# Two graph layers on one core: queries' sums as seven products of combined quarters

## The chip, the cores and the metric

The kernel runs on one core of a Trainium2 chip. A core has five engines that each work through their own instruction list in order: TensorE (PE in the profile; its weight loads are shown as PEld), VectorE (DVE), ScalarE (ACT), GpSimd (POOL) and SyncE (SP), which here only issues DMAs. The metric is the device time of one execution, in microseconds.

## The reference, cut to what matters

The input `x` is 16 graphs of 1024 nodes with 256 channels, `adj` one 1024 x 1024 matrix shared by all. The first layer, with `fea` the normed input with channels first:

```python
c_adj = jnp.mean(fea, axis=1)
diff = c_adj[:, None, :] - c_adj[:, :, None]
A = jnp.abs(jnp.abs(jax.nn.sigmoid(diff) - 0.5) - 0.5) * 2.0
A_s = (A + jnp.transpose(A, (0, 2, 1))) * 0.5
Wg = adj[None, :, :] * A_s
g = jnp.einsum('bcn,bnm->bcm', fea, Wg)          # <- the queries' sums
g = jax.nn.relu(g * para.reshape(1, C, N))
q = jnp.transpose(g, (0, 2, 1)).reshape(B, N, h, hd).transpose(0, 2, 1, 3)
kv = (x @ kv_w).reshape(B, N, 2, h, hd).transpose(2, 0, 3, 1, 4)
...
attn = jax.nn.softmax(jnp.einsum('bhnd,bhmd->bhnm', q, k) * scale, axis=-1)
out = jnp.einsum('bhnm,bhmd->bhnd', attn, v)
```

For each graph the 256 x 1024 matrix `g` is a product of the 256 x 1024 features with a 1024 x 1024 weighted graph `Wg`, which is different for every graph. The second layer multiplies the normed sum by a normalised adjacency (`A_hat`, the same for all graphs), then by W1, takes a batch norm over all graphs, a ReLU, W2, and a second batch norm.

## The kernel before

`layers(False)` does the first layer and the second up to W1; `second("f")` does the batch norms, W2 and the output. (`layers(True)` and `second("s")` are a safer path that is taken only if a sum of exponentials overflows; it doesn't run on this data.) All matrices are FP32.

**The order of the work.** The program is recorded in the order in which the code emits it, with no reordering, and every engine keeps that order. `attention` (line 806) walks over 16 graphs of 16 steps each. A step emits, in this order: `scores` of one group of nodes (`sc`, two PSUM tiles, and the exponentials `p` on ScalarE), the transposes of a finished unit (`ot`), additions of `p` into `acc` on VectorE, the products with the values of the step before (`o`), at the end of a unit the `sums` with four reciprocals on VectorE, and then pieces of a background. The background of graph b, `background(b)` at line 612, is a generator; it makes the queries, keys and values of graph b + 1, the gathering with `A_hat` (`aggregate`, PE `pa`) and W1 (`hidden`, PE `py`) of graph b - 1, and the norm and the weights' start (`prepare`) of graph b + 2. Each `yield 1.71` is one piece of TensorE work of that many microseconds; a step takes pieces until the sum of costs reaches the share of `total` (line 822) that is due. `weave` puts side generators beside a main one, one piece of each side per piece of the main. `soon(action)` emits an action after the next piece. A piece that yields `TOP` stops the step, and the next one begins with the background directly behind the scores.

**The queries.** `weigh` (line 363) makes `Wg` in 8 pieces of 256 rows x 512 columns (two row blocks of 128; 4 KB per partition). Piece i goes by two slots: in the first the DMA of `adj` for piece i + 1 is issued, VectorE finishes piece i - 1 (line 381, `w * adj`) and ScalarE begins piece i (line 394, two instructions), in the second ScalarE takes the tanh (line 402). `AHEAD = 6` slots run ahead of `queries`, the others beside it, one for each of its pieces. `queries` (line 407) multiplies each piece with both halves of the channels (k = 0, 1) into two PSUM banks, over the eight row blocks, for the left and then the right half of the columns: 2 x 8 x 2 = 32 products of 128 x 128 by 128 x 512. `product` splits each into two matmuls of 64 columns of weights; the profile shows two instructions for each matmul. At the end of a half VectorE multiplies by `para` (line 432) and ScalarE takes the ReLU (line 435). The pieces live in four buffers (`w`), as do those of `adj`, and the pieces of `A_hat` that `aggregate` loads are in the `adj` buffers too.

**The seven products.** `aggregate` already works with seven products of quarters: `graph` makes, once, from the normalised adjacency the four blocks and three combinations, in DRAM (`aht_d`), and `combine` and the functions behind each product combine quarters of the features and add the results. `h` is normed features, `h_a` for the first layer, `h_b` for the second; its quarters are a11, a12 (first channels, first and second half of the nodes) and a21, a22.

**The buffers around it.** `load_adj` and `load_adj_t` load pieces of `adj`; `columns_of` and `broadcast_row` make a row of 1024 values out of a column by transposes (tiles `cb`, PSUM `cbp`); `dbc` is such a row of the degrees, for `graph`. PSUM tiles of all these products are the two banks of `ps_mm` (`bank`, line 142). `y` tiles hold W1's results on the way to DRAM, in four buffers of the pool `py`. W2 (`w2`) is loaded in `degrees` (line 206) into memory of its own.

The head of the run, before `attention`, makes the keys, values and queries of graph 0:

```python
run(weave(keys_values(0), (8 - AHEAD, islice(weighers[0], AHEAD))))
load_x(1)
run(weave(queries(0), (0, weighers[0]), (5, Norm(1, True).all())))
attention()
run(aggregate(B - 1), hidden(B - 1))
```

## Time and profile before

| what | value |
|---|---|
| median of 3 runs | 2697.38 us (2697.13 to 2699.46) |
| the profiled execution, whole | 2699.94 us |
| its span in the profile | 2698.1 us |
| TensorE clock granted, mean | 0.988 |
| `pg` matmuls (queries' sums), busy | 457.1 us, 2048 instructions |
| `pa` matmuls (`aggregate`), busy | 346.0 + 57.8 us, 1536 + 256 instructions |
| one graph of the steady part (graphs 2 to 13) | 148.3 us |
| head, up to the first scores | 61.9 us |
| first product of the second part | begins at 2422.2 us |

The span is what lies between the first and the last recorded instruction of that execution. An engine's busy time is the sum of its instructions; in a row of a group the columns are the code's line, the engine, the operation, what it writes and reads, the shapes, the count, the busy time, the mean duration in nanoseconds, and the idle time of that engine just before such instructions with what ended it.

### The profile page before, as it was taken

The numbers are of one execution on the slowest core, as the hardware profiler recorded it, in microseconds if no ns is written. First come the engines' busy times: TensorE is split into PE (matmuls) and PEld (weight loads), VectorE is DVE, ScalarE is ACT, GpSimd is POOL, SyncE is SP. The second block draws the span as 40 slices with busy tenths as digits, with TensorE's granted clock in tenths as the row PEclk, the third lists the DMA queues.
The fourth block names the chain that finished last, engine by engine and source line by source line (L and its number), as shares of the span: only waits on it lengthen the run. The fifth ranks groups of instructions, "written<-read, shape, count | busy, mean of one in ns | idle before, by whom it ended". The sixth has DMA issues, their size and how long they took to land.

```text
span 2698.1 us, 32021 instructions
## 1 busy us (share of the span) xinstructions
PE 2620.7 (97%) x12106; PEld 968.3 (36%) x12106; DVE 1742.3 (65%) x2624; ACT 1292.3 (48%) x1845; POOL 363.2 (13%) x428
## 2 busy tenths in 40 slices
PE   7999999999999999999999999999999999989994
PEld 3333333333333333333333333333333333324443
DVE  5767666666666656666666666566666666656675
ACT  5653444536363544445363635444453634335544
POOL 0016000000000100000000001000000001026653
PEclk9999999999999999999999999999999999999997
DMA  4416414243332424142423324241424213355549
GB/s 156 159 58 225 161 53 164 86 148 103 107 116 98 141 80 158 51 168 83 150 100 109 114 98 141 84 155 51 168 82 152 99 63 118 113 215 187 202 182 364
DMA packets 128613, 355.05 MB, mean 132 GB/s; under 512 B 11969, under 2 KB 32961, under 8 KB 122305
## 3 DMA queue, kind: packets, MB, share of 16 engines
q1 hardware_dynamic: 109120, 278.44, 30.3%
q0 software_dynamic: 19328, 74.46, 7.3%
q8 instruction: 98, 1.61, 0.2%
q14 instruction: 67, 0.54, 0.1%
HBM read 278.41 MB, written 74.45 MB: 131 GB/s over the span
## 4 chain that ended last, share of the span: by engine, by line
PE 93%; DMA 3%; DVE 2%; issue 2%; ACT 1%; POOL 0%; SPq 0%; POOLq 0%; DVEq 0%; ACTq 0%
PE sc L704 18%; PE o L745 18%; PE pg L149 16%; PE pa L149 13%; PE py L149 7%; PE m_f L1017 7%; PE pk L149 4%; PE pv L149 4%; PE sums L762 2%; DMA out_dram<-xo_f 2%; PE ot L798 1%; PE htp L352 1%; PE cbp_c L192 1%; DMA y_d<-y 0%; DVE acc L734 0%
## 5 line engine op out<-in xcount | busy, mean ns | idle before, releaser
L712 ACT ACTIVATE p<-sc 128x1024 f32<-128x1024 f32 x512 | 496.4, 1021 | 700.8 <-PE sc L704 700.6
L734 DVE TENSOR_TENSOR acc<-acc,p 128x1024 f32<-128x1024 f32 x384 | 471.2, 1227 | 133.8 <-ACT p L712 112.5
L704 PE MATMUL sc<-q,k 64*128 64x512 f32 x2048 | 510.6, 617 | 0.5 <-ACT p L712 0.5
L745 PE MATMUL o<-p,v 128*64 128x512 f32 x2048 | 496.1, 605 | 0.0
L149 PE MATMUL pg<-w,h_a 128*64 128x512 f32 x2048 | 457.1, 596 | 7.5 <-DVE q L432 7.5
L149 PE MATMUL pa<-aht,h_b 128*64 128x512 f32 x1536 | 346.0, 592 | 2.7 <-DMA aht<-aht_d 2.7
L704 PEld LDWEIGHTS sc<-q,k 64*128 64x128 f32 x2048 | 176.6, 186 | 321.9 <-issue 270.3
L149 PEld LDWEIGHTS pg<-w,h_a 128*64 128x64 f32 x2048 | 148.2, 138 | 301.8 <-issue 281.7
L771 DVE RECIPROCAL inv<-sums 128x128 f32<-128x128 f32 x256 | 223.7, 921 | 24.6 <-PE sums L762 24.6
L149 PE MATMUL py<-at,w 128*64 128x512 f32 x1024 | 230.8, 592 | 2.1 <-ACT y L564 2.1
L745 PEld LDWEIGHTS o<-p,v 128*64 128x64 f32 x2048 | 124.3, 136 | 286.1 <-issue 285.9
L394 ACT ACTIVATE w<-cbc,csum 128x512 f32<-128x512 f32 x256 | 170.2, 714 | 74.3 <-PE pg L149 74.2
L731 DVE TENSOR_TENSOR acc<-p,p 128x1024 f32<-128x1024 f32 x64 | 78.5, 1226 | 194.8 <-ACT p L712 194.8
L381 DVE SCALAR_TENSOR_TENSOR w<-w,adj 128x1024 f32<-128x1024 f32 x128 | 156.5, 1223 | 54.7 <-ACT w L402 54.7
L149 PEld LDWEIGHTS pa<-aht,h_b 128*64 128x64 f32 x1536 | 110.6, 137 | 216.6 <-issue 204.9
L564 ACT ACTIVATE y<-py,vec 128x512 f32<-128x512 f32 x128 | 87.6, 684 | 188.4 <-PE py L149 155.1
L565 POOL DMA_DIRECT2D y_d<-y x128 | 70.7, 553 | 685.1 <-ACT y L564 681.9
L402 ACT ACTIVATE w<-w 128x1024 f32<-128x1024 f32 x128 | 134.8, 1053 | 1.7
L149 PEld LDWEIGHTS py<-at,w 128*64 128x64 f32 x1024 | 74.0, 137 | 147.8 <-issue 131.3
L149 PE MATMUL pv<-kvw,ht 128*64 128x256 f32 x1024 | 116.2, 379 | 0.4 <-DVE v L469 0.4
L82 POOL TENSOR_SCALAR lnsm_b<-mv_b 128x4 f32<-128x4 f32 x32 | 7.3, 230 | 805.2 <-DVE mv_b L277 805.1
L802 DVE TENSOR_TENSOR x<-ot,x 128x512 f32<-128x512 f32 x64 | 44.2, 691 | 110.6 <-PE ot L798 109.8
(133 smaller groups left out, 2526.4 us busy)
## 6 DMA issues: line engine op xcount, KB each, us to landing
aht<-aht_d SPq DMA_DIRECT2D x224, 512.0 KB, 4.2
adj<-in_adj_dram SPq DMA_DIRECT2D x128, 512.0 KB, 4.2
y_d<-y POOLq DMA_DIRECT2D x128, 256.0 KB, 2.8
yin_f<-y_d SPq DMA_DIRECT2D x32, 1024.0 KB, 6.3
x<-in_x_dram SPq DMA_DIRECT2D x32, 512.0 KB, 4.7
para<-in_para_dram SPq DMA_DIRECT2D x64, 256.0 KB, 4.1
x_d<-x POOLq DMA_DIRECT2D x16, 1024.0 KB, 4.2
xo_f<-x_d SPq DMA_DIRECT2D x32, 512.0 KB, 8.5
```

The lines of the kernel that those rows point to most:

```text
L149: nc.tensor.matmul(dst[r], left[:, r], right, start=start, stop=stop)
L381: nc.vector.scalar_tensor_tensor(w, w, 1.0, a, op0=ALU.add, op1=ALU.mult)
L394: nc.scalar.activation(w[:, t, :], cbc[:, q * FB : (q + 1) * FB], AF.Abs, bias=csum[:, th * TH + t : th * TH + t + 1], scale=-1.0,)
L402: nc.scalar.activation(made[i], made[i], AF.Tanh, scale=-0.5 / C)
L564: nc.scalar.activation(y, made, AF.Identity, bias=b1[:, j : j + 1])
L704: nc.tensor.matmul(sc[:, e, :], ks[b][k][r, m * P : (m + 1) * P], qs[b][k][r, f * FB : (f + 1) * FB], start=True, stop=True,)
L712: nc.scalar.activation(pr, sc, AF.Exp)
L731: nc.vector.tensor_add(self.acc, self.held, pr)
L734: nc.vector.tensor_add(self.acc, self.acc, pr)
L745: nc.tensor.matmul(self.o[r, :], vs[b][k][:, m, r], pr[:, e, :], start=(m == 0), stop=(m == NT - 1),)
L771: nc.vector.reciprocal(self.inv[:, c], self.pt[:, c])
L1017: nc.tensor.matmul(made, left[:, j, :], right[:, j, :], start=(j == 0), stop=(j == JH - 1))
```

## The change

`queries` now computes the four quarters of `g` (two halves of the channels, two halves of the columns) from seven products of a combined quarter of the features with a combined quarter of `Wg`, four row blocks each: 28 products in place of 32. The quarters of `Wg` are four blocks of two pieces each; the combinations are made in place, over the pieces and over the quarters of h_a, by `take`, `combine` and the functions `first` to `seventh`, on GpSimd, for graphs 0 and 2 on VectorE. All eight pieces are held at once (pool `p8`, tag `w`), which `aggregate` now uses for its loads too, five ahead instead of three. Beside this, `adj` has three buffers instead of four, `cb` uses the `y` buffers, `dbc` an `ht` buffer, and W2 is loaded at the start of the second part. The weights are made two slots per piece of the main generator (`double`), with `AHEAD = 9`. The background of graph 0 is put in another order, with the keys and values ahead of the queries, and `load_x(2)` moves to the head.

```diff
     nc.sync.dma_start(out=vec, in_=vecs)
-    w2 = const.tile([P, HC, C], F32, name="w2")
     b1, g1, be1 = (vec[:, i * HC : (i + 1) * HC] for i in range(3))
...
         p3 = st.enter_context(tc.tile_pool(name=f"p3_{kind}", bufs=3))
+        p8 = st.enter_context(tc.tile_pool(name=f"p8_{kind}", bufs=8))
         p4 = st.enter_context(tc.tile_pool(name=f"p4_{kind}", bufs=4))
...
+        def double(slots):
+            for _ in slots:
+                next(slots, None)
+                yield 0.0
         def bank(name):
...
         def load_adj(q, th, name):
-            t = p4.tile([P, TH, FB], F32, tag="adj", name=name)
+            t = p3.tile([P, TH, FB], F32, tag="adj", name=name)
             nc.sync.dma_start(
...
         nc.sync.dma_start(out=kvw, in_=kv_w.rearrange("(k p) j -> p k j", p=P))
-        dbc = big.tile([P, N], F32, name="dbc")
-        w1 = big.tile([P, CC, H1], F32, name="w1")
         rows = big.tile([P, NH, NT], F32, name="rows")
...
             for g in range(NT // 4):
-                cb = p2.tile([P, 4, P], F32, tag="cb", name=f"cb_{name}_{g}")
+                cb = py.tile([P, 4, P], F32, tag="y", name=f"cb_{name}_{g}")
                 nc.vector.tensor_copy(
...
         def load_adj_t(t, name):
-            tile_ = p4.tile([P, N], F32, tag="adj", name=f"{name}_{t}")
+            tile_ = p3.tile([P, N], F32, tag="adj", name=f"{name}_{t}")
             nc.sync.dma_start(out=tile_, in_=adj_t[t * P : (t + 1) * P, :])
...
         deg_sm = big.tile([P, 6, NT], F32, name="deg")
+        w1 = big.tile([P, CC, H1], F32, name="w1")
         row, diag, col, deg, tmp_deg, dinv = (deg_sm[:, i, :] for i in range(6))
...
             nc.sync.dma_start(out=w1, in_=w1_t.rearrange("(k p) j -> p k j", p=P))
-            nc.sync.dma_start(out=w2, in_=w2_t.rearrange("(k p) c -> p k c", p=P))
             nc.vector.tensor_reduce(row, rows.rearrange("p q t -> p t q"), AX.X, ALU.add)
...
-        def graph():
+        def graph(dbc):
...
                     cols = slice(part * HB, (part + 1) * HB)
-                    a = p4.tile([P, 2, NH, HB], F32, tag="adj", name=f"au_{t}_{part}")
+                    a = p3.tile([P, 2, NH, HB], F32, tag="adj", name=f"au_{t}_{part}")
                     for n in range(2):
...
                         load()
-                    w = p4.tile([P, TH, FB], F32, tag="w", name=f"w_{b}_{q}_{th}")
+                    w = p8.tile([P, TH, FB], F32, tag="w", name=f"w_{b}_{q}_{th}")
                     made.append(w)
...
-        AHEAD = 6
+        AHEAD = 9
+        def quarters(tag, b):
+            h = hs[tag, b]
+            HT = NT // 2
+            return [h[:, n * HT : (n + 1) * HT, c * P : (c + 1) * P] for c in (0, 1) for n in (0, 1)]
+        def combine(tag, b, engine):
+            a11, a12, a21, a22 = quarters(tag, b)
+            s1s[tag, b] = p1.tile([P, NT // 2, P], F32, tag="s1", name=f"s1_{tag}_{b}")
+            engine.tensor_add(s1s[tag, b], a21, a22)
+            engine.tensor_sub(a21, a11, a21)
...
-            h = hs["a", b]
+            engine = nc.vector if b in (0, 2) else nc.gpsimd
+            combine("a", b, engine)
+            a11, a12, a21, a22 = quarters("a", b)
+            s1 = s1s["a", b]
             qs[b] = [p4.tile([P, N], F32, tag="q", name=f"q_{b}_{k}") for k in range(CC)]
...
+            c11, c12, c21, c22 = (
+                qs[b][k][:, q * FB : (q + 1) * FB] for k in range(CC) for q in range(NH)
+            )
+            paras = {}
+            def load_para(k, q):
+                paras[k, q] = p2.tile([P, FB], F32, tag="para", name=f"para_{b}_{k}_{q}")
+                nc.sync.dma_start(
+                    out=paras[k, q], in_=para[k * P : (k + 1) * P, q * FB : (q + 1) * FB]
+                )
+            def finish(k, q):
+                dst = qs[b][k][:, q * FB : (q + 1) * FB]
+                nc.vector.tensor_mul(dst, dst, paras[k, q])
+                soon(lambda: nc.scalar.activation(dst, dst, AF.Relu, scale=SCALE))
+            add = nc.vector.tensor_add
+            load_para(0, 0)
+            HP = NP // 2
+            w = weighted[b]
+            def block(i):
+                return w[i * HP : (i + 1) * HP]
+            def take(i, x, y):
+                for dst, left, right in zip(block(i), block(x), block(y)):
+                    engine.tensor_sub(dst, left, right)
+            def first(m):
+                nc.scalar.copy(c12, m)
+                nc.scalar.copy(c21, m)
+                engine.tensor_sub(a11, s1, a11)
+            def second(m):
+                add(c11, m, c12)
+                engine.tensor_sub(a12, a12, a11)
+                take(0, 2, 0)
+                soon(lambda: finish(0, 0))
+            def third(m):
+                add(c22, m, c21)
+                take(2, 3, 2)
+                take(0, 3, 0)
+                load_para(0, 1)
+            def fourth(m):
+                add(c12, m, c22)
+                take(1, 1, 0)
+                load_para(1, 1)
+            def fifth(m):
+                add(c21, m, c21)
+                add(c22, m, c22)
+            def sixth(m):
+                for c in (c12, c22, c21):
+                    add(c, m, c)
+                soon(lambda: finish(0, 1))
+                soon(lambda: finish(1, 1))
+                soon(lambda: load_para(1, 0))
+            def seventh(m):
+                add(c21, m, c21)
+                soon(lambda: finish(1, 0))
+            for i, (left, right, after) in enumerate(
+                (
+                    (a11, 0, first),
+                    (a12, 1, second),
+                    (s1, 0, third),
+                    (a12, 3, fourth),
+                    (a21, 2, fifth),
+                    (a11, 0, sixth),
+                    (a22, 1, seventh),
+                )
+            ):
+                made = bank(f"pg_{b}_{i}")
+                for th in range(HP):
+                    for j in range(TH):
+                        t = th * TH + j
+                        product(
+                            made,
+                            left[:, t, :],
+                            w[right * HP + th][:, j, :],
+                            t == 0,
+                            t == NT // 2 - 1,
+                        )
+                    if th == HP - 1:
+                        after(made)
+                    yield 1.71
...
-        def quarters(b):
-            h = hs["b", b]
-            HT = NT // 2
-            return [h[:, n * HT : (n + 1) * HT, c * P : (c + 1) * P] for c in (0, 1) for n in (0, 1)]
-        def combine(b):
-            a11, a12, a21, a22 = quarters(b)
-            s1s[b] = p1.tile([P, NT // 2, P], F32, tag="s1", name=f"s1_{b}")
-            nc.vector.tensor_add(s1s[b], a21, a22)
-            nc.vector.tensor_sub(a21, a11, a21)
         def aggregate(b):
...
                     i = order[i]
-                    a = p4.tile([P, TH, FB], F32, tag="adj", name=f"aht_{b}_{i}_{th}")
+                    a = p8.tile([P, TH, FB], F32, tag="w", name=f"aht_{b}_{i}_{th}")
                     nc.sync.dma_start(out=a, in_=aht_d[i, th])
...
-            load(2)
+            load(4)
             yield 0.0
-            a11, a12, a21, a22 = quarters(b)
-            s1 = s1s[b]
+            a11, a12, a21, a22 = quarters("b", b)
+            s1 = s1s["b", b]
             at = ats[b] = [
...
                     n = i * NP // 2 + th
-                    load(n + 3)
+                    load(n + 5)
                     for j in range(TH):
...
             yield from Norm(b, False).all()
-            combine(b)
+            combine("b", b, nc.vector)
             nc.gpsimd.dma_start(out=x1_d[b], in_=xs[b])
...
                 yield from norm.half(half * NT // 2)
-            combine(B - 1)
+            combine("b", B - 1, nc.vector)
             nc.gpsimd.dma_start(out=x1_d[B - 1], in_=xs[B - 1])
...
             for k in range(CC):
-                yield from weave(islice(products, 3), (0, islice(w, 3)))
+                yield from weave(islice(products, 3), (0, double(islice(w, AHEAD // 2 + k))))
                 yield TOP
...
-        endings = []
+        def broadcast_dinv(cbs):
+            dbc = p3.tile([P, N], F32, tag="ht", name="dbc")
+            broadcast_row(dbc, cbs, "deg")
+            return dbc
+        endings, whole = [], []
...
-            nothing = iter(())
             if b == 0:
-                yield from prepare(1, nothing)
-                yield from weave(queries(1), (0, weighers[1]), (1, degrees()))
+                differences_1 = columns_of(csums[1], "c1")
+                yield TOP
+                differences(1, differences_1)
+                yield 1.0
+                for k in range(CC):
+                    yield TOP
+                    transposed(1, k)
+                    yield 1.0
+                w = weighers[1]
+                products = keys_values(1)
+                norm = Norm(2, True).all()
+                yield from weave(
+                    islice(products, 5), (0, double(islice(w, AHEAD))), (0, islice(norm, 5))
+                )
+                yield from weave(queries(1), (0, double(w)), (0, norm), (1, degrees()))
                 cbs = columns_of(dinv, "deg")
-                if B > 2:
-                    load_x(2)
-                    yield from weave(keys_values(1), (1, Norm(2, True).all()))
-                else:
-                    yield from keys_values(1)
+                yield from islice(products, 1)
                 yield TOP
-                broadcast_row(dbc, cbs, "deg")
+                whole.append(broadcast_dinv(cbs))
                 yield 1.0
-                if B > 2:
-                    yield from prepare(2, nothing)
+                yield from prepare(2, products)
                 return
...
             if b + 1 < B:
-                whole = graph() if b == 1 else nothing
-                yield from weave(queries(b + 1), (0, weighers[b + 1]), (0, whole))
+                sides = [(0, graph(whole.pop()))] if b == 1 else []
+                yield from weave(queries(b + 1), (0, double(weighers[b + 1])), *sides)
                 yield next(gather)
...
                         bg, done = background(b), 0.0
-                        total = 41.0 * (b + 1 < B) + 24.0 * (b > 0) + 6.0 * (b + 2 < B)
+                        total = 37.6 * (b + 1 < B) + 24.0 * (b > 0) + 6.0 * (b + 2 < B)
                         total += 13.7 * (0 < b < B - 2) + 27.4 * (b == B - 1) + 3.0 * (b == 0)
...
                     transposed(0, k)
-                run(weave(keys_values(0), (8 - AHEAD, islice(weighers[0], AHEAD))))
+                run(weave(keys_values(0), (2, double(islice(weighers[0], AHEAD)))))
                 load_x(1)
-                run(weave(queries(0), (0, weighers[0]), (5, Norm(1, True).all())))
+                load_x(2)
+                run(weave(queries(0), (0, double(weighers[0])), (4, Norm(1, True).all())))
                 attention()
...
         with st:
+            w2 = wp.tile([P, HC, C], F32, name="w2")
+            nc.sync.dma_start(out=w2, in_=w2_t.rearrange("(k p) c -> p k c", p=P))
             JH = HC // 2
```

More of the change, by code (lines that the diff above doesn't have):

```diff
@@ L407, in queries @@
         def queries(b):
-            h = hs["a", b]
+            engine = nc.vector if b in (0, 2) else nc.gpsimd
+            combine("a", b, engine)
+            a11, a12, a21, a22 = quarters("a", b)
+            s1 = s1s["a", b]
             qs[b] = [p4.tile([P, N], F32, tag="q", name=f"q_{b}_{k}") for k in range(CC)]
-            for q in range(NH):
-                cols = slice(q * FB, (q + 1) * FB)
-                pgs = [bank(f"pg_{b}_{q}_{k}") for k in range(CC)]
-                paras = []
-                for k in range(CC):
-                    paras.append(p2.tile([P, FB], F32, tag="para", name=f"para_{b}_{q}_{k}"))
-                    nc.sync.dma_start(out=paras[k], in_=para[k * P : (k + 1) * P, cols])
-                for th in range(NP):
-                    i = q * NP + th
-                    for k in range(CC):
-                        for j in range(TH):
-                            t = th * TH + j
-                            product(
-                                pgs[k],
-                                h[:, t, k * P : (k + 1) * P],
-                                weighted[b][i][:, j, :],
-                                t == 0,
-                                t == NT - 1,
-                            )
-                        if th == NP - 1:
-                            dst = qs[b][k][:, cols]
-                            nc.vector.tensor_mul(dst, pgs[k], paras[k])
-                            soon(
-                                lambda dst=dst: nc.scalar.activation(
-                                    dst, dst, AF.Relu, scale=SCALE
-                                )
-                            )
-                        yield 1.71
@@ L878, in layers @@
                         run(degrees())
-                        broadcast_row(dbc, columns_of(dinv, "deg"), "deg")
-                        run(graph())
+                        run(graph(broadcast_dinv(columns_of(dinv, "deg"))))
                     run(keys_values(b))
@@ L884, in layers @@
                     run(norm.all())
-                    combine(b)
+                    combine("b", b, nc.vector)
                     nc.gpsimd.dma_start(out=x1_d[b], in_=xs[b])
```

## The prediction

> **What bounds the kernel now.** I read the page's engine table first, then busy time by stage, then the chain of waits, then the groups of instructions with shapes kept apart, and last the timeline of one graph and of the passage between the two parts. The engine table:
>
> ```profile
> PE 2620.7 (97%) x12106; PEld 968.3 (36%) x12106; DVE 1742.3 (65%) x2624; ACT 1292.3 (48%) x1845; POOL 363.2 (13%) x428
> ```
>
> 97% is an average. By stage (columns: stretch, its length, busy time of PE, PEld, DVE, ACT, POOL, clock, DMA share, GB/s):
>
> ```profile
> 0.00:61.90 61.90, 47.11 (x250) 20.83 (x250) 34.15 (x69) 34.62 (x66) 5.89 (x16) 1.00 0.48 162
> 196.60:345.00 148.40, 142.01 (x670) 50.12 (x668) 103.85 (x156) 64.88 (x96) 56.26 (x70) 0.97 0.55 188
> 789.80:938.10 148.30, 148.30 (x716) 52.90 (x712) 95.38 (x143) 71.23 (x104) 10.07 (x17) 1.00 0.34 114
> ```
>
> The last line is one of twelve equal periods (graphs 2 to 13 in attention, while the queries of the graph after are made). TensorE has no gap there at all: a matmul taken out is worth its full time, and a wait put in costs its full time. GpSimd is almost idle, 10 us of 148. In the second line GpSimd and VectorE build the seven graph pieces and PE has 6.4 us of gaps already.
>
> In the chain of waits the work to be changed stands so (start, us, what):
>
> ```profile
> 789.82 6.87 PE pg L149 x32
> 800.48 5.15 PE pg L149 x24
> ```
>
> 6.87 / 32 = 0.2147 us for each of the profile's `pg` instructions (it shows two for each matmul of the code). The prices of the other operations, from the groups with their shapes (mean ns after the comma):
>
> ```profile
> L381 DVE SCALAR_TENSOR_TENSOR w<-w,adj 128x1024 f32<-128x1024 f32 x128 | 156.5, 1223 | 54.7 <-ACT w L402 54.7
> L1005 POOL TENSOR_TENSOR t_f<-yin_f,t_f 128x1024 f32<-128x1024 f32 x15 | 46.4, 3090 | 6.4 <-PE m_f L1017 5.8 <-PE good_f L1162 0.5
> L432 DVE TENSOR_TENSOR q<-pg,para 128x512 f32<-128x512 f32 x64 | 44.1, 689 | 62.6 <-PE pg L149 62.1
> L1002 POOL TENSOR_TENSOR t_f<-yin_f,yin_f 128x1024 f32<-128x1024 f32 x15 | 35.4, 2363 | 0.0
> L963 POOL TENSOR_TENSOR combined<-w 128x256 f32<-128x256 f32 x1 | 0.7, 725 | 0.0
> ```
>
> So GpSimd takes 2.36 us for a difference of 128x1024, against 1.22 us for VectorE's operation of that size. For 128x512 on GpSimd there is no row: between 0.725 (256) and 2.363 (1024) the slope is 2.13 ns per element, so I estimate 0.725 + 256 x 0.00213 = 1.27 us. Why L1005 takes 3.09 and L1002 2.36 is in the timeline (start, us, engine):
>
> ```profile
> 2448.74 1.21 DVE L1009 TENSOR_TENSOR yin_f<-yin_f 128x1024 f32<-128x1024 f32 x1
> 2449.12 3.05 POOL L1005 TENSOR_TENSOR t_f<-yin_f,t_f 128x1024 f32<-128x1024 f32 x1 [0.47 <-PE m_f L1017]
> ```
>
> The GpSimd operation is 0.69 us longer; VectorE's ended 0.83 us after it began. It simply waited for it.
>
> **What the Trainium skill says.** "SBUF — State Buffer", Who interferes with whom: VectorE with two SBUF inputs and a GpSimd operation that reads SBUF exclude each other for a whole instruction; with one input in PSUM they don't. The two lines above agree, and operations with PSUM inputs (L1046 beside L1012, 2.36 us) cost nothing. "GPSIMD Engine Reference", Performance versus the Vector engine, has GpSimd 1.96 times slower for two inputs; here it is 2363/1223 = 1.93.
>
> **The change part by part.**
>
> *Removed.* 32 products of one row block become 28: per graph 16 instructions of 0.2147, 3.43 us; 16 graphs, 55 us. The built program has 896 instead of 1024 `pg` matmuls, so this does happen.
>
> *Added beside other work.* Per graph: 9 VectorE additions from PSUM and 4 multiplications by `para` (13 x 0.69 = 9.0) in place of 4 (2.75): +6.2; two ScalarE copies (0.585 each): +1.2; 4 GpSimd combinations of 128x512 (1.27) and 8 of 128x1024 (2.36): 24 us. VectorE goes from 95 to 102 of 148, ScalarE to 72, GpSimd to 34. As totals all are hidden; as latencies not.
>
> *The new wait (the main term).* In the built order of a steady graph TensorE has: product 1, half of product 2, scores, values, the other half of product 2, and straight after it product 3. Product 3 reads block 0 after `take(0, 2, 0)`. On GpSimd that stands behind `a12 - a11` in `second`, which may not begin before product 2 has read a12. So from the end of product 2 TensorE waits for 1.27 + 2.36 and about 0.3 for three hand-overs: 3.9 us. The second piece of block 0 comes 2.36 after the first, while half of product 3 takes 16/2 x 0.2147 = 1.72: another 0.64. Bare cost 4.6 us, already above the 3.43 saved. TensorE takes its instructions in order; scores of the next step, which could fill the gap, stand behind.
>
> Then the lock. ScalarE now makes a piece of weights in one step (0.67 + 0.67 + 1.05) instead of half a piece, and the two copies. Laid out from the steady start (933.4 in the trace before; product 2 would end at 948.4) its queue is full from 937.8, so the exponentials of the second pair end about 948.4 and 949.4, and VectorE's two `acc` additions (1.23 each, two SBUF inputs) fall just where GpSimd wants to start; then come the last weighing (1.22) and the `para` product (0.69). Taking turns: if `acc` goes first, 1.2 wait, 1.27, 1.23 wait, 2.36, 0.2: product 3 is 6.3 late, and its second half 1.9 more (1.22 of weighing between the pieces): 8.2. If GpSimd goes first: 1.27 + 1.2 + 2.36 + 0.3 = 5.1, and 1.9: 7.0. Bounds 4.6 to 8.2; I take 7.0. The later pieces (blocks 2, 0, 1 for products 5 to 7) end about 18 to 30 us after product 2 and are wanted after 18 to 33: no further wait, though little to spare. Net 12 x (7.0 - 3.43) = +43.
>
> Graph 15 is made at another pace: product 3's halves lie in two steps, so only 6.3 or 5.1 counts: +3. Graph 1 has scores, transposes and values between products 2 and 3 (about 4.4 us), so little wait there.
>
> *Weighing at double pace in `prepare`.* Its first four and five slots go out two per product. ScalarE then has, in one step of three `py` products (5.15 us), 2.4 for each of two pieces, three `y` (0.68) and before, in the next, exponentials. The transposes of h_a need the PSUM bank of the third `py`, freed by a `y` that now stands behind two pieces: by the timeline at 911 and 922, 0.5 and 1.0 us late. Bounds 0 and 1.8 per graph; I take 1.2, thirteen times: +16.
>
> *Head (graph 0).* Combinations on VectorE: +2 x 0.69 for `combine`, +2 x 0.69, 8 x 1.22, and +6.2: 18.7 us on an engine that in the head also has eight weighings with row sums (2.43 each). Product 3 waits for seven of these, about until 52 where products 1 and 2 are done at 41; then `take` after `take`. I get the first scores at about 70 instead of 61.9: +8 (3 to 12).
>
> *Graph 1, in the background of graph 0.* Keys and values now come first with double weighing and the norm of graph 2; ScalarE has some 3 us per 1.72 us step and exponentials stand behind it: 7 us of gaps against 3.43 saved: +4 (-3 to +8). *Graph 2*: combinations on VectorE, in the stage that already has gaps, with three instead of four `adj` buffers for the graph's loads: +5 (0 to +12).
>
> *Passage to the second part.* The W2 load moves from early on SP's queue to the front of the second part, where its space was used before by the `y` tiles; it waits for the last store of `y`:
>
> ```profile
> 2401.12 34.45 SPq L973 DMA_DIRECT2D yin_f<-y_d  x6
> 2418.93 0.54 POOL L565 DMA_DIRECT2D y_d<-y  x1 [0.68 <-ACT y L564]
> 2421.26 5.75 ACT L979 ACTIVATE yin_f<-yin_f,sm 128x512 f32<-128x512 f32 x8 [2.63 <-DVE sm L919]
> ```
>
> The last store is issued at 2418.9 and takes 2.8 (the page's issue table), so 2421.7; the four `yin` loads behind it on SP, which ran from 2401, start only then, and the first lands 6.3 later: first ReLU at about 2428.5 instead of 2421.3, +7. The longer run of `aht` loads ahead takes away the 2.7 us that PE waited for `aht`. Net +4.
>
> Sum: 43 + 3 + 16 + 8 + 4 + 5 + 4 = +83. The profiled execution took 2699.9 (span 2698.1 and 1.8 around it), so 2783; the median of the runs lies 2.6 lower, and I say 2778, rounded down since the smaller terms have been read high more easily than low.
>
> **The rivals.** A, as above: 2778, chance 0.56.
> B, no lock loss and ScalarE keeps up: 12 x (4.6 - 3.43) = 14, graph 15 +1, head +5, passage +4, the rest about +4: +28, 2725. For it: GpSimd and VectorE may interleave better than I laid out. Against: both `acc` and the weighing are due in just this stretch. 0.22.
> C, the bursts make ScalarE and VectorE late as well: delayed `acc` hold up `sums`, exponentials hold up scores; 8.2 per graph and 2 to 3 more: 12 x 7.5 = 90, prepare 23, head and graphs 1 and 2 at their upper ends 30, others 7: +150 at the extreme; 2825 taken. Against: sums over a period leave ScalarE and VectorE a third idle. 0.15.
> D, not slower: the wait before product 3 is below the saving. This is decided at a wait of 3.43 us. It would need GpSimd's two operations to last what VectorE's do (0.69 + 1.22 + 0.3 = 2.2, second piece hidden): 14 x (2.2 - 3.43) = -17, other terms nil, 2680. Sixteen savings with no wait at all would be 2642. The 2.36 us row speaks against it, and nothing for it but that DVE and ScalarE have room. 0.07.
>
> **How the numbers follow.** Likeliest A, 2778. A's own terms and the larger part of B and of C are in 2720 to 2825; outside lie D and the far end of C. A measurement of this kernel can tell about 0.2% (5.4 us) from no change. Only D and a sliver of B lie near or below it: faster 0.06, same 0.02, slower 0.92.
>
> **What would show it.** In the profile after: `pg` x1792 in place of x2048; the wait of the `pg` line in steady periods on POOL, some 5 to 8 us per graph in two pieces of about 5 to 6 and 1 to 2; GpSimd's 128x1024 differences at 2.4 to 3.6 us; the steady period at 152 to 154 instead of 148.3; first scores near 70; first `m_f` near 7 us later after the last `y` store. I am wrong if the period is below 148.3: then product 3 does not wait as long as GpSimd's chain. If the wait is there but the transposes in `prepare` don't wait, only that term falls.

## The result and the profile after

The changed kernel takes 2825.35 us (median of 4 runs, 2822.95 to 2826.34); the kernel before took 2698.27 beside it (2697.13 to 2699.46). The ratio is 1.047, 95% interval 1.0451 to 1.0488. The direction was forecast; the loss is 127 us where 80 were forecast. The span grew from 2698.1 to 2824.2, by 126.1.

Engine table of the page after (busy us, share, instructions):

```profile
PE 2612.4 (93%) x11850; PEld 952.8 (34%) x11850; DVE 2003.7 (71%) x2792; ACT 1305.7 (46%) x1877; POOL 766.1 (27%) x596
```

TensorE does 8.3 us less than before, not 55 less: some of its work became slower. VectorE is 261 us busier.

Busy time by stage of the kernel after (stretch, length, PE, PEld, DVE, ACT, POOL, clock, DMA share, GB/s): head, background of graph 0, background of graph 1, one period of an equal graph:

```profile
0.00:77.70 77.70, 48.66 (x232) 20.95 (x232) 50.48 (x89) 35.43 (x68) 5.90 (x16) 0.91 0.36 118
77.70:213.79 136.09, 115.40 (x539) 42.59 (x537) 102.56 (x133) 78.94 (x118) 33.72 (x18) 0.94 0.26 88
213.79:382.90 169.11, 150.78 (x697) 52.31 (x696) 134.99 (x193) 74.74 (x110) 60.31 (x72) 0.96 0.53 177
852.25:1006.85 154.60, 147.65 (x699) 51.95 (x696) 111.71 (x153) 72.11 (x106) 38.30 (x29) 0.98 0.32 109
```

The clock column is lowest in the first two, where it stood at 1.00 and 0.99 before. The stages are cut at the first scores of each graph (and at the first `m_f`), read from TensorE's timeline, in us. "Twelve" is the backgrounds of graphs 2 to 13, "per graph" a twelfth of it; "rest" ends with TensorE's last instruction, 29 to 30 us before the span does:

| kernel | head | graph 0 | graph 1 | twelve | per graph | graph 14 | graph 15, passage | rest |
|---|---|---|---|---|---|---|---|---|
| before | 61.9 | 118.1 | 160.4 | 1779.2 | 148.27 | 131.6 | 171.1 | 246.8 |
| after | 77.7 | 136.1 | 169.1 | 1857.4 | 154.78 | 135.1 | 172.3 | 247.0 |
| take_first | 77.4 | 133.1 | 168.6 | 1771.7 | 147.64 | 130.1 | 172.0 | 249.3 |
| no_differences | 67.6 | 122.5 | 162.0 | 1769.2 | 147.43 | 128.2 | 171.9 | 247.0 |
| all_on_vector | 78.7 | 126.4 | 169.1 | 1845.0 | 153.75 | 134.3 | 171.7 | 247.5 |
| both_edits_plain_0_1 | 62.9 | 117.3 | 167.0 | 1755.0 | 146.25 | 131.3 | 171.6 | 246.8 |

So of the 126 us, 78 are in the equal graphs and 42 in the head and graphs 0 and 1. The groups of instructions of the kernel after, shapes apart (count, busy us, mean ns, idle time ahead and what ended it):

```profile
L155 PE MATMUL pg<-w,h_a 128*64 128x512 f32 x1536 | 345.6, 595 | 6.2 <-DVE q L488 2.4 <-DVE q L482 1.6 <-DVE v L555 1.0
L155 PE MATMUL pg<-w,s_a 128*64 128x512 f32 x256 | 89.7, 858 | 86.3 <-POOL w L462 67.9 <-DVE w L462 18.4
L155 PE MATMUL py<-at,w 128*64 128x512 f32 x1024 | 231.0, 593 | 14.7 <-DVE ht L359 14.7
L356 PE MATMUL htp<-ident,h_a 128*128 128x128 f32 x256 | 41.6, 292 | 10.5 <-ACT y L635 10.5
L462 POOL TENSOR_TENSOR w<-w,w 128x1024 f32<-128x1024 f32 x112 | 327.0, 2952 | 1.2 <-DVE w L385 1.2
L817 DVE TENSOR_TENSOR acc<-acc,p 128x1024 f32<-128x1024 f32 x384 | 557.9, 1453 | 94.3 <-ACT p L795 74.3
```

`pg` is x1536 + x256 = 1792: the products did go. Only product 3 reads `s_a`, and ahead of it stand 86.3 us of wait; the `py` and `htp` lines are the waits in `prepare`. A difference on GpSimd takes 2.95 us on average, not the 2.36 of an undisturbed one, and VectorE's `acc` addition 1453 ns instead of 1227: they take turns. One equal graph, timeline of GpSimd and then of TensorE (start, us, engine):

```profile
863.06 1.52 POOL L471 TENSOR_TENSOR h_a<-h_a 128x512 f32<-128x512 f32 x1 [5.94 <-PE pg L155]
864.55 9.37 POOL L462 TENSOR_TENSOR w<-w,w 128x1024 f32<-128x1024 f32 x3
```

```profile
861.02 1.89 PE L155 MATMUL pg<-w,h_a 128*64 128x512 f32 x8
867.92 5.58 PE L155 MATMUL pg<-w,s_a 128*64 128x512 f32 x16 [5.01 <-POOL w L462]
```

Product 2 ends at 862.9; GpSimd begins `a12 - a11` then and its first difference at 864.55. Product 3 stands 5.0 us, and then takes 5.5 until the next scores instead of 16 x 0.2147 = 3.4; the granted clock is 0.50 from 865.01 to 871.84.

### The profile page after: what moved, and what is told of

It is laid out like the page before. It is cut to its first block, busy times and chain, and to the rows that moved or that the text cites. A ratio compares the mean times of both kernels' runs of the same rounds, so it can differ in the third digit from the quotient of the medians.

```text
span 2824.2 us, 32108 instructions
## 1 busy us (share of the span) xinstructions
PE 2612.4 (93%) x11850; PEld 952.8 (34%) x11850; DVE 2003.7 (71%) x2792; ACT 1305.7 (46%) x1877; POOL 766.1 (27%) x596
## 3 DMA queue, kind: packets, MB, share of 16 engines
q8 instruction: 96, 1.57, 0.2%
## 4 chain that ended last, share of the span: by engine, by line
PE 77%; DVE 7%; ACT 5%; issue 5%; DMA 3%; POOL 3%; SPq 0%; POOLq 0%; ACTq 0%; DVEq 0%
PE o L828 15%; PE sc L787 15%; PE pg L155 13%; PE pa L155 13%; PE m_f L1102 7%; PE py L155 4%; PE pv L155 3%; PE pk L155 3%; ACT w L398 3%; DMA out_dram<-xo_f 2%; PE sums L845 2%; POOL w L462 2%; ACT y L635 1%; DVE w L385 1%; PE ot L881 1%
## 5 line engine op out<-in xcount | busy, mean ns | idle before, releaser
L817 DVE TENSOR_TENSOR acc<-acc,p 128x1024 f32<-128x1024 f32 x384 | 557.9, 1453 | 94.3 <-ACT p L795 74.3
L787 PE MATMUL sc<-q,k 64*128 64x512 f32 x2048 | 510.9, 617 | 11.4 <-ACT p L795 11.4
L155 PE MATMUL pg<-w,h_a 128*64 128x512 f32 x1536 | 345.6, 595 | 6.2 <-DVE q L488 2.4
L462 POOL TENSOR_TENSOR w<-w,w 128x1024 f32<-128x1024 f32 x112 | 327.0, 2952 | 1.2 <-DVE w L385 1.2
L385 DVE SCALAR_TENSOR_TENSOR w<-w,adj 128x1024 f32<-128x1024 f32 x128 | 179.5, 1404 | 104.1 <-ACT w L406 101.6
L155 PE MATMUL py<-at,w 128*64 128x512 f32 x1024 | 231.0, 593 | 14.7 <-DVE ht L359 14.7
L81 POOL TENSOR_SCALAR lnsm_a<-mv_a 128x4 f32<-128x4 f32 x32 | 7.2, 226 | 678.9 <-DVE mv_a L281 678.9
L155 PEld LDWEIGHTS pg<-w,h_a 128*64 128x64 f32 x1536 | 111.1, 137 | 226.6 <-issue 212.8
L814 DVE TENSOR_TENSOR acc<-p,p 128x1024 f32<-128x1024 f32 x64 | 91.9, 1435 | 118.1 <-ACT p L795 118.1
L155 PE MATMUL pg<-w,s_a 128*64 128x512 f32 x256 | 89.7, 858 | 86.3 <-POOL w L462 67.9
L449 ACT ACTIVATE q<-q 128x512 f32<-128x512 f32 x64 | 39.8, 630 | 192.3 <-DVE q L447 192.3
```

The lines of the kernel that those rows point to most:

```text
L155: nc.tensor.matmul(dst[r], left[:, r], right, start=start, stop=stop)
L385: nc.vector.scalar_tensor_tensor(w, w, 1.0, a, op0=ALU.add, op1=ALU.mult)
L462: engine.tensor_sub(dst, left, right)
L787: nc.tensor.matmul(sc[:, e, :], ks[b][k][r, m * P : (m + 1) * P], qs[b][k][r, f * FB : (f + 1) * FB], start=True, stop=True,)
L817: nc.vector.tensor_add(self.acc, self.acc, pr)
```

## The experiments

**1. The wait before product 3: take_first.**

```diff
 def first(m):
     engine.tensor_sub(a11, s1, a11)
+    soon(lambda: take(0, 2, 0))
 def second(m):
     engine.tensor_sub(a12, a12, a11)
-    take(0, 2, 0)
```

> Edit: on GpSimd the two differences of block 0 (take(0, 2, 0)) stand before a12 - a11 and no longer behind it; nothing else changes. Theory 1 (product 3 waits because the two differences cannot begin until product 2 has read a12, though they need only pieces 4 and 5 weighed): they now run while product 2 runs, the wait before product 3 (5.0 us, and 2.1 more inside it, per graph) falls to 0 to 1, the steady period from 154.8 to 147 to 149, the total by 75 to 95 us, to 2730 to 2750. Rival (the lock only moves: the differences now hold up the acc additions and the last weighing, and scores or product 3 wait for these): the period falls by 1 to 3 us only, total 2785 to 2815, with new waits of PE on ScalarE or VectorE. Rival (pieces 4 and 5 are weighed too late for it): the wait stays above 3 us, with a VectorE weighing as the last releaser.

Measured: 2734.32 us, ratio to before 1.0132 (1.0116 to 1.0149). TensorE's timeline at the same place has no wait:

```profile
835.56 1.89 PE L155 MATMUL pg<-w,h_a 128*64 128x512 f32 x8
837.28 3.60 PE L155 MATMUL pg<-w,s_a 128*64 128x512 f32 x16
```

The period falls by 7.14 us, to 147.64. Theory 1 holds: two instructions in the wrong order on one queue cost 91 us. The lock did move (`acc` 1508 ns), but it hit nothing that TensorE waits for in these graphs. Head and graph 0 hardly moved: their loss is another.

**2. No differences, and all on VectorE.**

```diff
 def take(i, x, y):
-    for dst, left, right in zip(block(i), block(x), block(y)):
-        engine.tensor_sub(dst, left, right)
+    pass
```

> Left out: the eight 128x1024 differences of weighted pieces per graph (take), on both engines; products 3, 5, 6 and 7 read the plain pieces, so the queries are another sum. The order of the products, the combinations of h and the additions stay. Theory 1 (these differences, by their wait and by the lock on VectorE, are most of the loss): steady period 147 to 148, head to the first scores about 70 instead of 77.7, background of graph 0 about 122 instead of 136, total 2700 to 2725. Rival (head and graph 0 are late because of the new order of keys, values, norm and double weighing): the steady period falls alike, but head and graph 0 stay within 3 us of 77.7 and 136, total 2730 to 2745.

```diff
-engine = nc.vector if b in (0, 2) else nc.gpsimd
+engine = nc.vector
```

> Edit: the combinations of all graphs on VectorE, as the kernel has them in graphs 0 and 2. Theory 1 (GpSimd's pace and its lock against VectorE are the price): an operation takes 1.22 instead of 2.36 to 2.95 us and needs no turn; the wait before product 3 falls from 7.1 to about 4.5 us per graph and the 9.6 us stop of graph 0's scores goes; total 2770 to 2790. Rival (VectorE is one queue: acc additions, weighing and para products now stand behind eight differences): what product 3 gains is lost in scores and sums, total 2815 to 2850.

Measured without the differences: 2699.08 us, ratio 1.0004 (0.9995 to 1.0013). Of the head's +15.8 they are 10.1, of graph 0's +18.0 they are 13.6; the rest (5.7 and 4.4) stays, so both theories hold a part. The sober reading is the equal graph: 147.43, that is 0.84 below before where 3.43 of products were removed. So 2.59 us per graph go to something that is neither product 3's wait nor the differences. As placed, the change would gain nothing even if differences were free.

All on VectorE: 2803.22 us, ratio 1.0387 (1.037 to 1.0405), better than the changed kernel by 22 and between the two theories. The equal graph gains only 1.03 of the expected 2.6 (product 3 still waits 4.37 us, behind VectorE's own queue). Graph 0's background falls by 9.7. The reason is in the kernel after, around a stop of its scores; VectorE, GpSimd, ScalarE and TensorE from the timelines of the engines:

```profile
135.88 6.34 DVE L817 TENSOR_TENSOR acc<-acc,p 128x1024 f32<-128x1024 f32 x2
142.15 2.42 DVE L218 TENSOR_TENSOR db<-at,ident 128x128 f32<-128x128 f32 x1
144.80 2.51 DVE L447 TENSOR_TENSOR q<-q,para 128x512 f32<-128x512 f32 x1
```

```profile
135.50 14.03 POOL L462 TENSOR_TENSOR w<-w,w 128x1024 f32<-128x1024 f32 x5 [1.23 <-DVE w L385]
```

```profile
147.35 0.63 ACT L449 ACTIVATE q<-q 128x512 f32<-128x512 f32 x1 [12.73 <-DVE q L447]
147.88 1.92 ACT L795 ACTIVATE p<-sc 128x1024 f32<-128x1024 f32 x2
```

```profile
148.94 2.08 PE L787 MATMUL sc<-q,k 64*128 64x512 f32 x4 [9.55 <-ACT p L795]
```

Five differences hold GpSimd for 14.03 us. In that time each VectorE operation with two SBUF inputs waits for one of them: a multiplication of 128x128 takes 2.42. The `para` product so ends at 147.3, ScalarE's ReLU behind it stands 12.7 us, the exponentials stand behind that ReLU, and the scores have no free bank: 9.55 us of TensorE. With all on VectorE the idle time of the `sc` line that ends on `p` falls from 11.4 to 1.8 us. In the kernel before, the `para` product read PSUM and took 689 ns on average (L432); the change gave it two SBUF inputs, and in the kernel after it takes 1158 (L447), with all on VectorE 695.

**3. `prepare`.**

```diff
-yield from weave(islice(products, 3), (0, double(islice(w, AHEAD // 2 + k))))
+yield from weave(islice(products, 3), (0, islice(w, AHEAD // 2 + k)))
```

> Edit: the weighing slots in prepare go out one per product again, four and five in the two groups of three products as before, not two per product; the rest stays. Theory 1 (the pair of slots puts two pieces of weights on ScalarE ahead of y, and the transposes htp wait for y, the next py for htp): both waits (0.8 and 1.1 us per graph) and their htp at lower pace go, 13 x 2 to 2.5 us, total 2793 to 2800. Rival (the slots left over, one and two, still stand together ahead of exponentials, or the waits come from VectorE's queue): less than 10 us gained, total 2815 to 2830, htp and py still waiting.

Measured: 2811.78 us, ratio 1.0418 (1.0401 to 1.0435): 13.6 us gained, 1.06 per equal graph, between the two theories. The `htp` wait is gone, the one of `py` grew from 14.7 to 17.5 us: the copies of `ht` stand on VectorE behind the leftover slots. So these slots were put after the transposes, on top of take_first:

```diff
 for k in range(CC):
-    yield from weave(islice(products, 3), (0, double(islice(w, AHEAD // 2 + k))))
+    yield from weave(islice(products, 3), (0, islice(w, 3)))
     ...
-yield from products
+yield from weave(products, (0, islice(w, AHEAD - 6)))
```

> Edit: take_first, and in prepare three slots and three beside the two groups of products, the other three with the last product, after the transposes. Theory 1 (the waits of htp and py come from ht copies and y standing behind weighing that was put out in pairs or as a leftover ahead of the transposes): both waits fall below 0.4 us per graph together, steady period from 147.6 to 145.2 to 146, total 2705 to 2715. Rival (the three slots left over now stand ahead of the first exponentials of the next graph, or the first products of the queries find no weighed pieces): 2720 to 2734, with new waits on sc or pg.

Measured: 2712.71 us, ratio 1.0056 (1.004 to 1.0071). Both waits are gone, and the period falls by 1.39 to 146.25:

```profile
L155 PE MATMUL py<-at,w 128*64 128x512 f32 x1024 | 230.3, 592 | 0.0
L356 PE MATMUL htp<-ident,h_a 128*128 128x128 f32 x256 | 36.0, 286 | 0.0
L155 PE MATMUL pg<-w,h_a 128*64 128x512 f32 x1536 | 345.0, 593 | 20.9 <-DVE q L471 12.8 <-DVE q L488 2.6 <-DVE q L482 2.1
```

The last line shows what is late next: 12.8 us, 0.97 per graph, ahead of product 4, whose bank VectorE's addition `q` L471 has not yet emptied. That is why the period ends just above theory 1's 145.2 to 146; the total is in its range.

**4. Head, graph 0, graph 1 in the old form.** Graphs 0 to 2 with the 32 products of the kernel before (`queries_plain` is its `queries`), head and background of graph 0 in the old order:

```diff
-run(weave(queries(0), (0, double(weighers[0])), (4, Norm(1, True).all())))
+run(weave(queries_plain(0), (0, weighers[0]), (5, Norm(1, True).all())))
...
-yield from weave(queries(b + 1), (0, double(weighers[b + 1])), *sides)
+if b == 1:
+    yield from weave(queries_plain(2), (0, weighers[2]), *sides)
```

> Edit: take_first, and graphs 0, 1 and 2 have their queries in the form of the kernel before (32 products of a row block, weighing one slot per product, the background of graph 0 and the head in the old order); graphs 3 to 15 as in take_first. The rest of the change (three adj buffers, eight pieces, W2 late) stays. Theory 1 (in the head and in graphs 0 and 1 it is the seven products with their differences that cost): head about 62, graph 0's background about 118, graph 1's about 160, total 2690 to 2700. Rival (three adj buffers instead of four, or the later W1 and dbc, cost there): 5 to 20 us of the 39 remain, with waits that end on DMA adj, total 2703 to 2720.

Measured: 2710.28 us, ratio 1.0043 (1.0027 to 1.0058). Head 63.0 and graph 0 118.1, as theory 1 says; graph 1 became worse, 177.1, where theory 1 has about 160. The total is in the rival's range, and the waits do end on DMAs, but on those of `au`. VectorE in graph 1, from its timeline:

```profile
207.01 1.37 DVE L243 TENSOR_TENSOR au<-au,dbc 128x512 f32<-128x512 f32 x2 [8.67 <-DMA au<-in_adj_t_dram]
221.86 0.29 DVE L242 TENSOR_TENSOR au<-au,ident 128x128 f32<-128x128 f32 x1 [8.49 <-DMA au<-in_adj_t_dram]
```

It stands twice for the loads of `au`, which share the three `adj` buffers and SP's queue with the weighing; behind it stood the `q` product for which TensorE waited 15.8 us. Which of the two, buffers or queue, these runs don't separate: a fourth buffer wasn't tried. With the `prepare` edit as well:

> The two kernels before this in one: take_first, plain queries for graphs 0 to 2, three slots and three and the rest in prepare. Theory 1 (they are independent): 2663 to 2678, faster than the kernel before. Rival (the prepare edit only moves the waits): 2685 to 2700, equal to it.

2693.73 us, ratio 0.9984 (0.9977 to 0.999): above the 2663 to 2678 of theory 1, mostly because graph 1 stays at 174.6, where it counted on 160. The period is 146.25, as with the `prepare` edit alone, so the `prepare` edit did not just move its waits. With graph 2 back in seven products, and three more of its weighing slots ahead of them:

> Edit: both_edits, but only graphs 0 and 1 have the queries of the kernel before; graph 2 has the seven products with its combinations on VectorE, as in the changed kernel. Theory 1 (graph 1's background is slow in both_edits, 174.6 us, since 32 products with weighing at one slot each wait for adj in three buffers that the build of the graph's pieces shares; with seven products it was 166 to 169): total 5 to 9 us less than both_edits, 2684 to 2690. Rival (the wait comes from the pieces' build itself and stays): 2691 to 2697.

2684.9 us, ratio 0.9951 (0.9938 to 0.9965), graph 1's background 167.0. This one beats both kernels, the one before by 13 us. Which of the two, the products or the earlier weighing, mended graph 1 wasn't separated.

**5. The turns that are left.** The 0.97 us ahead of product 4, in VectorE's timeline of both_edits_plain_0_1:

```profile
1242.76 5.57 DVE L852 TENSOR_TENSOR acc<-acc,p 128x1024 f32<-128x1024 f32 x2
1248.25 0.68 DVE L471 TENSOR_TENSOR q<-pg,q 128x512 f32<-128x512 f32 x1
```

Two `acc` additions take 5.57 us instead of 2.5, and `q` stands behind them. To take GpSimd out of it, the same kernel with `engine = nc.vector`:

> Edit: both_edits_plain_0_1 with all combinations on VectorE. Theory 1 (what is left of the loss in the equal graphs, 0.97 us of wait on VectorE's q ahead of product 4, comes from acc additions that take turns with GpSimd's differences, 5.6 us for two): without GpSimd there are no turns, the wait goes, the period falls from 146.25 to 145 to 145.5, total 10 to 15 us below both_edits_plain_0_1. Rival (one queue: eight differences of 1.22 us ahead of acc and of the q additions hold up as much): no gain, or the period above 147 and the total 10 to 40 us above.

Measured: 2709.78 us, ratio 1.0043 (1.0029 to 1.0056), 25 us worse; the rival is right. The `q` wait is gone, but product 3 waits again, 2.51 us, behind VectorE's queue, and the period is 148.27:

```profile
1105.78 3.65 PE L155 MATMUL pg<-w,s_a 128*64 128x512 f32 x16 [2.51 <-DVE w L462]
1253.35 5.35 PE L155 MATMUL pg<-w,s_a 128*64 128x512 f32 x16 [2.51 <-DVE w L462]
```

**6. The clock after a gap.** The two lines above differ only in TensorE's speed. Work that nobody needs was put into the gap, in the equal graphs and, in another run, in the head (`b == 0`, ten times):

```diff
 made = bank(f"pg_{b}_{i}")
+if i == 2 and 3 <= b < B - 1:
+    for _ in range(6):
+        product(made, s1[:, 0, :], w[HP][:, 0, :], True, True)
```

> Edit to the changed kernel: in the twelve equal graphs, six more products (24 of the profile's pg instructions, 5.15 us at 0.2147) into product 3's own bank ahead of its real start, from s1 and a piece of block 1 that is ready; the start of product 3 overwrites them, so the result stays. They fill the time in which TensorE waits. Theory 1 (the clock that is lost in the 5 us gap is paid in full: product 3 takes 5.5 us instead of 3.43): with the gap filled the clock stays up and the period falls by 1.0 to 2.1 us although TensorE gets 5.15 us more work, total 2800 to 2813. Rival (the slow first half of product 3 only fills the wait for the second piece of block 0, which comes 2.4 to 3 us after the first): the period falls by less than 0.7, total 2816 to 2825, product 3's halves at 1.7 us each with a wait of 1 us or more between. Third (the gap is shorter than the filler in some graphs): slower than 2825.

> Edit to the changed kernel: in graph 0 alone, ten more products (40 pg instructions, 8.6 us) into product 3's own bank before its real start, in the 9.4 us in which TensorE waits in the head. Theory 1 (after such a gap TensorE runs at a lower clock for some us: product 3's 16 instructions took 5.38 us): product 3 takes 3.4 to 3.7 us and the first scores come 1.5 to 2 us sooner than the 77.4 to 79.6 of the runs so far, although TensorE does 8.6 us more. Rival (product 3 is slow because its second piece comes late): its 16 instructions keep a gap and take 5 us or more.

Equal graphs: 2820.79 us, 4.6 below the changed kernel, 0.50 us per graph. Head: 2821.99 us, first scores at 76.01 instead of 77.70. TensorE's timelines of the two kernels:

```profile
862.80 7.16 PE L155 MATMUL pg<-w,s_a 128*64 128x512 f32 x32
871.31 1.94 PE L155 MATMUL pg<-w,s_a 128*64 128x512 f32 x8 [1.35 <-POOL w L462]
```

```profile
43.31 8.78 PE L155 MATMUL pg<-w,s_a 128*64 128x512 f32 x40
53.26 3.65 PE L155 MATMUL pg<-w,s_a 128*64 128x512 f32 x16 [1.16 <-DVE w L462]
66.36 5.35 PE L155 MATMUL pg<-w,h_a 128*64 128x512 f32 x16 [2.58 <-DVE q L482]
72.43 3.65 PE L155 MATMUL pg<-w,h_a 128*64 128x512 f32 x16 [0.72 <-DVE q L488]
```

In the equal graphs (first fence; x32 is the 24 added and product 3's first half) the rival is right: at full speed product 3 only waits longer for its second piece. In the head theory 1 is right about product 3: after 9.40 us of idleness it took 5.38, now 3.65, although TensorE does more work. The 1.7 us at the first scores are less sure: they come from one trace, and the same head without the added work gave 77.70 to 79.58 us in four (the kernel after, all_on_vector, filler, prepare_single_pace).

## Why the prediction was right or wrong

Measured over stages, against its own terms:

| term | predicted | measured |
|---|---|---|
| product 3 in twelve graphs, net | 12 x (7.0 - 3.43) = +43 | 12 x (7.14 - 3.43) = +44.5 (take_first) |
| graph 15's queries | +3 | +3.5 |
| `prepare`, per graph | 1.2, bounds 0 and 1.8 | 2.4 in the twelve: waits 0.8 and 1.1, longer transposes 0.4 (take_first) |
| head | +8 (3 to 12) | +15.8 (up to 17.7 in other traces of the same head) |
| graph 1, in the background of graph 0 | +4 (-3 to +8) | +18.0 |
| graph 2, and one `prepare` | +5 and 1.2 | +8.7 |
| passage | +4 | +1.4 with all after it |

**Right:** the main term, in its cause and in its sum, though the sum came out so close partly by luck. The order on GpSimd (`take` behind `a12 - a11`), the 1.27 us for 128x512 (L424 takes 1.272), the lock and `pg` x1792 were as read, and moving the two instructions took away just the 7 us priced. Of these, 5.0 are the wait, as laid out with GpSimd first (5.1). The other 1.9 were priced as a wait for the second piece. In the kernel after there is no such wait; product 3 ran at half the clock instead, of which the prediction has nothing. At full clock (the equal graphs of section 6) the wait is there, 1.35 us, and the period is only 0.5 shorter: the one hides the other. The first `m_f` came late, its wait 11.7 us instead of 4.8, about the 7 forecast. Against it stand the wait for `aht` that went as forecast (2.7) and one of `py` for `y` that went unforecast (2.1), so the passage lost less than 4. The equal graph came out at 154.8, above the stated 152 to 154, mostly by the `prepare` term.

The total is the 2825 of rival C almost to the digit, and that is luck. C puts 90 us into the equal graphs beside `prepare`, where about 49 were measured, and 30 into the head and graphs 1 and 2, where 42 were.

**Wrong, "Graph 1, in the background of graph 0: +4".** This step failed by 14 us, in kind. It counted 7 us of gaps from ScalarE's load, net +4. Without the differences graph 0's background is 4.4 us longer than before, about that; the other 13.6 are the differences', to which the term gave nothing. What came was rival C's mechanism in one place: GpSimd's run of differences locks VectorE, whose `para` product is ahead of ReLU, exponentials and scores; all_on_vector took 9.7 of the 18.0 away. The prediction had laid the lock out only for the wait before product 3. It never asked what else on VectorE meets the later differences, which it had called "no further wait" in the steady graphs. And it priced the `para` products at 0.69 us, the price with an input in PSUM, which they no longer have.

**Wrong, "Head: +8".** TensorE's timeline of the head in the kernel after:

```profile
52.54 5.38 PE L155 MATMUL pg<-w,s_a 128*64 128x512 f32 x16 [9.40 <-DVE w L462]
66.35 3.65 PE L155 MATMUL pg<-w,h_a 128*64 128x512 f32 x16 [1.57 <-DVE q L482]
72.42 5.35 PE L155 MATMUL pg<-w,h_a 128*64 128x512 f32 x16 [2.41 <-DVE q L488]
```

Product 3's start was read rightly (about 52; it is 52.54). Behind it, products 6 and 7 wait 1.57 and 2.41 us for additions on VectorE. These stand behind `take` and behind the statistics of graph 1's norm, the last of which itself waits for GpSimd, 0.61 us ahead of product 6's addition and 1.47 ahead of product 7's:

```profile
70.91 0.16 DVE L292 SCALAR_TENSOR_TENSOR lnsm_a<-mv_a,lnsm_a 128x4 f32<-128x4 f32 x1 [1.47 <-POOL lnsm_a L82]
```

Two of the products run at the lower clock, 5.38 and 5.35 us instead of 3.43. Waits and clock make 4.0 + 3.9 = 7.9, which is the miss. No run separates the norm's share from that of `take`. The Trainium skill, "TensorE: Matmul & The Clock Gate", Part 1, says that an idle window of about 3.4 us puts the array back to half rate (here 2.41 us of idleness were enough, see the last section); the prediction made gaps and didn't price the restart. The trace before had shown one: after 4.72 us idle, eight `pg` instructions took 3.68 us instead of 1.9.

**Mis-sized, "`prepare`: I take 1.2".** The term is right in mechanism (the waits went with the slots) and was 2.4. It counted how late `y` frees the bank for the transposes, 0.8 us, but not that the next `py` then waits for the copies of `ht`, 1.13, nor that the transposes themselves then take longer: `htp` is busy for 41.6 us in the kernel after and for 36.0 without the pairs of slots, 0.4 for each of thirteen graphs. Mending it gave 1.39 a graph, since the wait ahead of product 4 came up in its place.

## What to carry to other kernels

Before pricing an added operation, look at where its queue puts it: what its result needs may be ready long before its turn, and one moved line was worth 91 us of the 127 here. An operation that locks another engine has to be followed beyond its own consumer: list every instruction of the locked engine in that time, and who waits behind each. And a kernel whose bound engine has no gaps needs all followers of a saving in place: with two placements mended and the first two graphs left alone, the same idea gives 0.5% instead of costing 4.7%.

## What the runs showed of the hardware

TensorE's lower clock needs less idleness than expected. After gaps of 0.72, 1.16 and 1.57 us, 16 `pg` instructions took 3.65 us; after 2.41 (head of the kernel after) and 2.58 us, 5.35; after 2.42 us in the head of take_first_prepare_3_3_rest, 3.65. After 2.51 us in both_edits_plain_0_1_vector they took 3.65 in seven of the twelve equal graphs and 5.35 in five.

The granted clock that the traces record explains the two outcomes. In each trace it changes only on a grid of 3.41 us, and how long TensorE is busy in one stretch of that grid tells the clock in the next. For the two gaps of 2.51 us shown in section 5, the stretches are (columns as in the stages above):

```profile
1103.83:1107.25 3.42, 1.47 (x8) 0.73 (x10) 3.42 (x4) 1.10 (x2) 0.00 (x0) 1.00 0.00 0
1250.61:1254.02 3.41, 0.90 (x6) 0.40 (x6) 3.41 (x4) 1.89 (x3) 0.00 (x0) 1.00 0.04 16
```

The second holds its whole gap, TensorE is busy for 0.90 us, and the next stretch has clock 0.50. The first holds 1.95 us of its gap, TensorE is busy for 1.47, and the clock stays at 1.00. In all thirteen traces, each of the 153 full-clock stretches with less than 1.40 us busy was followed by one at half clock, and none of the 9800 with more than 1.68 was. The Trainium skill, "TensorE: Matmul & The Clock Gate", Part 1, says that the activity window runs freely, which agrees; but the window here need not be idle throughout.
